# Attention and a binarised convolution on 64x64 images: other tiles summed in DRAM, the next x in eight pieces, and another order of the row products

## The chip, the cores and the metric

The kernel runs on one core of a Trainium2 chip. The core has TensorE for matmuls (PE in the profile; PEld is its weight load), VectorE (DVE), ScalarE (ACT), GpSimd (POOL), and SyncE (SP), which here only issues transfers. SP and GpSimd each have their own queue of transfers. Times are device microseconds of one execution; lower is better. The kernel before takes 1929.31 us, the median of three runs (1928.18 to 1931.14).

## The reference

Two layers work on x of shape (8, 64, 64, 64): 8 images, 64 channels, 64x64 pixels.

```python
# layer 0: attention over the n = 4096 pixels of an image
q = wq @ xf + bq;  k = wk @ xf + bk;  v = wv @ xf + bv      # per image, (64, 4096)
q, k = q - mean(q), k - mean(k)
sim = softmax(q^T k / 8, over the keys)                     # (4096, 4096)
out = sim @ v^T + (a softmax-weighted mean of v, from mean(q) and k)
x = x + out
# layer 1: three binarised convolutions (1x1, 3x3, 5x5) with batch norm, then a gate
s = sum over k in (1, 3, 5) of bn_k(conv_k(sign(x + move_k), binarised w_k))
gate = sigmoid(grouped product of mean(s) + gb), its channels shuffled
return s * gate + x
```

## The kernel before

Two images stand in the 128 partitions, so there are four pairs. The queries of a pair are cut into eight blocks of 512, so there are 32 blocks, numbered g in the order of the run. The keys are cut into 32 tiles of 128. Every matrix product is issued on quarters of the array, 64x64, so that both images and both halves of the keys are worked on together.

One block is a loop over the 32 key tiles j, and one turn of it is called a slot here. In each slot `scores` makes the 512 scores per key for both images (L491) and ACT takes their exponential into a tile e (L502); `weighted` multiplies the e of the slot before with the values and adds it to the PSUM banks acc (L510); `summed` adds that same e to the running sum es on VectorE (L526, L528), which is later needed as the softmax's denominator. The tiles e come from a pool of five buffers. One of the five is held in the first slots of a block by `parts`, the gathered sums of the block before.

Not every e is added on VectorE. For the tiles in `DRAM_TILES` (L41), `add_in_dram` (L541) sends e to a tile in DRAM instead: the first by a plain write on SP's queue (L547), the others by an accumulating transfer on GpSimd's queue (L549). At the next block's start `send` adds es in the same way, and `gather` (L554) brings the total back on SP's queue; `fold_first`, `fold`, `fold_last` reduce it on VectorE to the reciprocal, and `spread` (L581) sends it through DRAM to all partitions as r. A buffer of e is free for a new exponential only when its matmul, and its addition or its transfer, have read it.

`plan(g)` (L1079) writes by hand what else is done in which slot: `put(i, f)` calls f in slot i, after that slot's scores and the slot before's `weighted` and `summed`. Each engine works strictly in the order in which it is given its instructions. So the order of `put` calls is the order on every engine and in every queue. The work of the convolution layer is spread over the following blocks: in block g, for block g-1, `added` (the two halves of acc, L609), `finish` (times r, plus the residual, L613 and L614), and the three signs (`signs_wide` L646 for the 5x5 and 3x3, `signs` L640 for the 1x1, ACT), in slots 12 to 19; for block g-2 the combinations of rows (`row_step`, slots 17 to 24, VectorE) and their copies (`row_copies`, SP's queue); for block g-3 the products of these rows.

Those products are in `mix_rows` (L981), which runs in slot 0. It makes next block's queries (L477) and then 40 products of the 5x5 and 18 of the 3x3 for each image (L798), plus the 1x1. A product is named (k, n, tap): for the 5x5, n = 4 and 5 are the points 1/2 and -1/2, n = 0 to 3 the points 1, -1, 2, -2, n = 6 and 7 the ends. Two sequences, one for each half of the array's rows, are merged by a clock. The 3x3's products lie in the banks acc, which must have been copied out first by `weighted_out` (L535 on ACT, L536 on VectorE). `hold` (L821) brings a bank to SBUF on ACT, `join` (L830) adds another to it on VectorE. When these are done the banks go back to scores and acc.

The next pair's x is loaded by `load_x` (L67) in four transfers of 512 KB on SP's queue, all in slot 1 of the pair's third block. Its column means are taken by ACT (`mean_part`, L288) in slots 14, 16, ... 28, of the fourth block in pair 0 and of the third block in the others. In blocks five to eight of a pair the next pair's values are made (`values`, `unary_part`), two groups in each; in the eighth also `unary_sum`. In the third and fourth block the pair before is stored (`store`, L927).

Of the kernel before, what the change touches and what calls it, by code (L numbers as in the profile page):

```python
# [18 lines left out]
F32 = mybir.dt.float32  # L19
# [7 lines left out]
P = 128  # L27
C = 64
HH = 64
N = HH * HH  # L30
# [7 lines left out]
BN_EPS = 1e-5  # L38
TAPS = [[(r, c) for r in range(k) for c in range(k)] for k in KS]
FIRST = [0, 1, 10, 35]  # L40
DRAM_TILES = (4, 9, 14, 19, 24, 28)  # L41
LOW, HIGH = 1e-20, 1e20


# [1 line left out]
def conv_seq_kernel(ctx, tc, x, wq, wk, wv, vecs, w1, w3, w5, wtap, gw, out):  # L46
    nc = tc.nc
    n_pairs = x.shape[0] * x.shape[1] // P
    xf = x.rearrange("b c h w -> (b c) (h w)")
# [4 lines left out]
    xp = ctx.enter_context(tc.tile_pool(name="xp", bufs=2))  # L54
# [9 lines left out]
    def m_tile(name):  # L64
        return ps_m.tile([P, QB], F32, tag="m", name=name)

    def load_x(name, rows, queues=(nc.sync,)):  # L67
        xt = xp.tile([P, N], F32, tag="x", name=f"x_{name}")
        for c in range(4):
            cols = bass.ts(c, N // 4)  # L70
            queues[c % len(queues)].dma_start(out=xt[:, cols], in_=xf[rows, cols])
        return xt
# [12 lines left out]
    xt = load_x("0", slice(0, P), (nc.sync, nc.scalar, nc.sync, nc.sync))  # L85
# [188 lines left out]
    class Pair:  # L274
# [266 lines left out]
        def add_in_dram(self, qb, e, first=False):  # L541
            if first:
                self.sent = self.tile(dp, "es", qb, (4, 32, 4, QB // 2))
            out = self.sent.rearrange("g i q c -> (g i) (q c)")
            e = e.rearrange("p b c -> p (b c)")
            if first:
                nc.sync.dma_start(out=out, in_=e)  # L547
            else:
                nc.gpsimd.dma_start(out=out, in_=e, accum_op=ALU.add)  # L549

# [430 lines left out]
    def mix_rows(q, c):  # L981


        seqs = [[], []]
        if q is not None:
            for h in range(2):
                seqs[h].append((("q",), 0, 2.0))
        if c is not None:
            p, (r0, _, y) = c
            qb = r0 // ROWS  # L990

            def products(k, *names):
                return [((k, n), i, 0.25) for n in names for i in range(k)]

            seqs[0] += products(5, 4) + products(3, 4, 5, 0, 1, 2, 3) + [((1,), 0, 1.0)] + products(5, 5)
            seqs[1] += products(5, 0, 1, 2, 3, 6, 7)
        order = []
        for h, seq in enumerate(seqs):
            at = 0.0
            for t in seq:  # L1000
                order += [(at, h, b, t) for b in (h, 1 - h)]
                at += t[2]
        order.sort(key=lambda o: o[0:2])
        if q is not None:
            q[0].query_tiles(q[1])
        left, acc, banks5, ends = {}, None, None, None
        for o in order:
            left[o[3][0]] = left.get(o[3][0], 0) + 1
        for _, h, b, (n, i, _) in order:
            if n == ("q",):  # L1010
                q[0].split_queries(q[1], b, h)
            elif n == (1,):
                if left[n] == 2:
                    p.z1 = m_tile(f"z{p.name}_{qb}_1")
                p.conv_tap((r0, ROWS, y), [[p.z1]], b, 0, 0, 0, True, True)
            else:
                if banks5 is None:
                    banks5 = score_banks(f"z{p.name}_{qb}_5")
                if n[0] == 3:
                    if acc is None:  # L1020
                        acc = acc_banks(f"z{p.name}_{qb}_3")
                    z = acc[n[1] // 4][:, bass.ts(n[1] % 4, 2 * HH)]
                elif n[1] in (4, 5):
                    z = banks5[0][:, bass.ts(n[1] - 4, 2 * HH)]
                elif n[1] < 4:
                    z = banks5[1][:, bass.ts(n[1], 2 * HH)]
                else:
                    if ends is None:
                        ends = m_tile(f"z{p.name}_{qb}_5e")
                    z = ends[:, bass.ts(n[1] - 6, 2 * HH)]  # L1030
                p.row_product(z, b, *n, i)
            left[n] -= 1
            if left[n] > 0:
                continue
            if n == ("q",):
                q[0].split_queries_out(q[1])
            elif n == (3, 5):
                p.hold(acc[1][:, 0 : 4 * HH], 6, 2, 0)
            elif n == (3, 3):
                p.hold(acc[0], 0, 4, 0)  # L1040
        if c is not None:
            p.hold(banks5[0][:, 0 : 4 * HH], 4, 2, 2)
            p.join(ends[:, 0 : 4 * HH], 6, 2)
            p.join(banks5[1], 0, 4)

# [20 lines left out]
    def rows_of(pr):  # L1066
        return slice(pr * P, (pr + 1) * P)

    def attend(pairs):
# [9 lines left out]
        def plan(g):  # L1079
# [4 lines left out]
            def put(i, f, *a):  # L1084
                at.setdefault(i, []).append((f, a))

            pr, qb = divmod(g, NQ)

            def nx():
                return pairs[pr + 1]  # L1090
# [32 lines left out]
            if g >= 1:  # L1123
                put(5, p.fold_first, b)
                put(6, p.fold, b)
                put(7, p.fold_last, b)
                put(8, p.spread, b)
                put(9, p.check_block, b, 0)
                put(11, p.check_block, b, 1)
                put(12, p.added, b)  # L1130
                put(13, p.finish, b)
                put(15, p.signs_wide, b, 2)
                put(17, p.signs_wide, b, 1)
                put(19, p.signs, b)
            if g + 2 < n_blocks:
                put(2, lambda: block(g + 2)[0].copy_x(block(g + 2)[1], (g + 2) // NQ * P))
            if 2 <= g < n_blocks - 1:
                p2, b2 = block(g - 2)
                for i in range(5):
                    put(17 + i, p2.row_step, b2, 5, i)  # L1140
                put(21, p2.row_copies, 5)
                for i in range(2):
                    put(22 + 2 * i, p2.row_step, b2, 3, i)
                put(24, p2.row_copies, 3)
            if g == n_blocks - 4:
                put(14, p.copy_tile)
# [23 lines left out]
            if pr + 1 < n_pairs:  # L1170
                if qb == 2:
                    def begin():
                        pairs[pr + 1] = Pair(str(pr + 1), load_x(str(pr + 1), rows_of(pr + 1)))

                    put(1, begin)
                if qb == (3 if pr == 0 else 2):
                    for c in range(8):
                        cols = slice(c * QB, (c + 1) * QB)
                        put(14 + 2 * c, lambda c=c, cols=cols: nx().mean_part(c, cols, True))
                    put(30, lambda: nx().mean_sum(8))  # L1180
                if qb >= 4:
                    for h in range(2):
                        i = 2 * (qb - 4) + h
                        put(14 + 8 * h, lambda i=i: nx().values(i))
                        put(17 + 8 * h, lambda i=i: nx().unary_part(i))
                    if qb == NQ - 1:
                        put(28, lambda: nx().unary_sum())
# [6 lines left out]
        for g in range(n_blocks):  # L1194
            pr, qb = divmod(g, NQ)
# [206 lines left out]
```

## Time and profile before

| what | value |
|---|---|
| median of three runs | 1929.31 us |
| the profiled execution | 1928.91 us, its span 1927.1 us, mean granted clock 0.995 |
| idle of ACT before L502, put down to DMA es<-e | 22.9 us in 8 times, 7.6 the longest |
| idle of VectorE before L564, put down to DMA e_parts<-es | 20.5 us in 12 times |
| transfers es<-e and es<-es on GpSimd's queue | 155 and 31, 512 KB each, 5.4 us to landing (median) |
| transfers es<-e on SP's queue | 31, 512 KB each |
| x<-in_x on SP's queue | 15, 512 KB each |
| an undisturbed block (block 11) | 57.47 us: TensorE busy 57.35, VectorE 47.50, ACT 38.63 |

A line of the profile names the engine, the line of the kernel, the operation, out<-in by the names of the tiles, and how many there were. In the list of groups, the numbers after the bar are the busy time, the mean of one in ns, and then the idle time of the engine just before them with what ended it. In a list of waits the numbers are us in total, times, and the longest. In the table of stretches each row is start:end, length, and then the busy time and number of instructions of PE, PEld, DVE, ACT and POOL, the granted clock of TensorE, the share of the DMA engines' time, and GB/s. TensorE's matmuls are pipelined and overlap, so their busy time is not their number times their length.

### The profile page before, as it was taken

To read this page: it belongs to the slowest core of one execution; us is meant where nothing else is said; L and a number is where in the kernel's file an instruction comes from. 1 tells how busy PE (TensorE), PEld (TensorE's weight loads), DVE (VectorE), ACT (ScalarE), POOL (GpSimd) and SP (SyncE) were. 2 spreads that over 40 slices of the span, in tenths; PEclk is the share of its full clock that TensorE was granted. 3 is DMA by queue.
4 is the path that set the end of the run, shared out by engine and by line. 5 is a ranking of instruction groups with operands and counts; after the bars stand their busy time and mean duration, and the time that the engine had idled before them with its cause. 6 is when DMAs were issued, how large, how long until landed. Compare 5 with 4: busy or idle time off the path is not lost.

```text
span 1927.1 us, 50314 instructions
## 1 busy us (share of the span) xinstructions
PE 1891.6 (98%) x21486; PEld 798.8 (41%) x21486; DVE 1517.0 (79%) x2423; ACT 1279.8 (66%) x1639; POOL 165.7 (9%) x208
## 2 busy tenths in 40 slices
PE   9999999999998999999999999999999999999997
PEld 4333444444343344444434444334443444444444
DVE  6768877878876788787887778887887888877886
ACT  5665776666665766666666676666666666666663
POOL 0000000010000100000100001000001000001000
PEclk9999999999999999999999999999999999999999
DMA  5454444444445554444444555444444445544421
GB/s 134 80 100 99 86 83 92 87 79 83 89 88 125 95 110 83 89 92 87 69 90 85 126 109 108 81 84 88 90 90 74 87 101 109 104 91 83 85 44 46
DMA packets 80223, 174.72 MB, mean 91 GB/s; under 512 B 11180, under 2 KB 41720, under 8 KB 79864
## 3 DMA queue, kind: packets, MB, share of 16 engines
q0 software_dynamic: 26816, 97.54, 32.2%
q1 hardware_dynamic: 52456, 72.71, 12.3%
q8 instruction: 170, 2.79, 0.6%
q10 hardware_dynamic: 720, 1.18, 0.2%
q14 instruction: 61, 0.50, 0.1%
HBM read 39.27 MB, written 122.29 MB: 84 GB/s over the span
## 4 chain that ended last, share of the span: by engine, by line
PE 49%; DMA 1%; DVE 1%; ACT 0%; issue 0%; SPq 0%; ACTq 0%
PE ps L491 23%; PE acc L510 23%; DMA es<-e 1%; PE z L798 1%; DVE o L536 1%; PE z L885 0%; PE z_5e L798 0%; ACT e L502 0%; PE pv L330 0%; PE pre L1243 0%; DVE r L603 0%; ACT rc_ck L435 0%; DVE es L528 0%; SPq L468 0%; PE su L596 0%
## 5 line engine op out<-in xcount | busy, mean ns | idle before, releaser
L502 ACT ACTIVATE e<-ps 128x1024 f32<-128x1024 f32 x1024 | 1049.1, 1025 | 590.9 <-PE ps L491 549.6
L528 DVE TENSOR_TENSOR es<-es,e 128x1024 f32<-128x1024 f32 x774 | 943.8, 1219 | 265.5 <-ACT e L502 260.3
L510 PE MATMUL acc<-e,v 64*64 64x512 f32 x8192 | 1089.8, 590 | 13.1 <-ACT e L502 12.9
L491 PE MATMUL ps<-q,x 64*64 64x512 f32 x8192 | 1093.1, 591 | 3.5 <-ACT e L502 2.6
L510 PEld LDWEIGHTS acc<-e,v 64*64 64x64 f32 x8192 | 333.7, 131 | 561.3 <-ACT e L502 321.5
L491 PEld LDWEIGHTS ps<-q,x 64*64 64x64 f32 x8192 | 350.1, 133 | 489.5 <-issue 346.3
L549 POOL DMA_DIRECT2D es<-e x155 | 133.7, 863 | 1499.5 <-ACT e L502 954.9
L865 DVE SCALAR_TENSOR_TENSOR sb<-pt,sb 128x256 f32<-128x256 f32 x174 | 65.9, 420 | 0.0
L798 PE MATMUL z<-t,wc 64*64 64x128 bf16 x1392 | 60.6, 217 | 3.9 <-DVE o L536 0.5
L798 PEld LDWEIGHTS <-wc 64*64 64x64 bf16 x3364 | 58.9, 106 | 11.7 <-issue 8.2
L798 PE MATMUL z<-ec,wc 64*64 64x128 bf16 x1392 | 61.6, 217 | 0.0
L828 ACT ACTIVATE pt<-z,frac 128x256 f32<-128x256 f32 (+1 forms) x87 | 44.3, 543 | 15.6 <-PE z L798 15.6
L526 DVE TENSOR_TENSOR es<-e,e 128x1024 f32<-128x1024 f32 x32 | 39.2, 1224 | 15.6 <-ACT e L502 15.6
L646 ACT ACTIVATE s<-x,vec 128x512 bf16<-128x512 f32 (+2 forms) x66 | 46.1, 702 | 5.6 <-DVE x L614 5.6
L833 DVE SCALAR_TENSOR_TENSOR pt<-z_5e,frac,pt 128x256 f32<-128x256 f32 x29 | 14.0, 484 | 41.1 <-PE z L798 38.0
L549 POOL DMA_DIRECT2D es<-es x31 | 26.8, 863 | 172.3 <-DVE es L528 156.7
L564 DVE TENSOR_TENSOR e_parts<-e_parts 128x512 f32<-128x512 f32 x31 | 21.4, 691 | 22.0 <-DMA e_parts<-es 20.5
L536 DVE COPY o<-acc 128x512 f32<-128x512 f32 (+2 forms) x33 | 22.2, 675 | 9.6 <-PE acc L510 9.6
L839 DVE TENSOR_TENSOR pt<-pt 128x384 f32<-128x384 f32 x58 | 29.6, 552 | 0.0
L330 PEld LDWEIGHTS pv<-wx,x 64*64 64x64 f32 x1024 | 22.4, 134 | 17.0 <-issue 10.6
L613 DVE TENSOR_TENSOR x<-x,r 128x512 f32<-128x512 f32 (+2 forms) x33 | 22.2, 671 | 8.2 <-DMA r<-rc 6.0
L614 DVE SCALAR_TENSOR_TENSOR x<-x,ou,x 128x512 f32<-128x512 f32 (+2 forms) x33 | 24.3, 736 | 1.2
(177 smaller groups left out, 859.6 us busy)
## 6 DMA issues: line engine op xcount, KB each, us to landing
es<-e POOLq DMA_DIRECT2D x155, 512.0 KB, 5.4
es<-e SPq DMA_DIRECT2D x31, 512.0 KB
es<-es POOLq DMA_DIRECT2D x31, 512.0 KB, 5.4
e_parts<-es SPq DMA_DIRECT2D x124, 128.0 KB
r<-rc SPq DMA_DIRECT2D x62, 128.0 KB
x<-in_x SPq DMA_DIRECT2D x15, 512.0 KB
out<-sb SPq DMA_DIRECT2D x28, 256.0 KB
xc<-in_x SPq DMA_DIRECT2D x60, 64.0 KB
```

The lines of the kernel that those rows point to most:

```text
L491: nc.tensor.matmul(ps[img[h], b, :], self.x[img[b], bass.ds(j * P + h * H, H)], self.q[qb][img[b], :], start=True, stop=neg is None,)
L502: nc.scalar.activation(e, ps, AF.Exp, scale=1.0 / 8.0)
L510: nc.tensor.matmul(self.acc[qb][h][img[b], :], self.v[img[h], j, img[b]], e[img[h], b, :], start=(j == 0), stop=(j == NK - 1),)
L526: nc.vector.tensor_tensor(self.es[qb], self.first, e, ALU.add)
L528: nc.vector.tensor_tensor(self.es[qb], self.es[qb], e, ALU.add)
L536: nc.vector.tensor_copy(self.acc[qb][1][:, c], acc[1][:, c])
L549: nc.gpsimd.dma_start(out=out, in_=e, accum_op=ALU.add)
L646: nc.scalar.activation(sy[n][0][:, rows, pad : pad + HH], self.x2[qb][:, r0 * HH : r1 * HH].rearrange("p (h w) -> p h w", w=HH), AF.Sign, ...
L798: nc.tensor.matmul(z[img[b], :].rearrange("p (q w) -> p q w", w=HH), wc[k][img[h], n, c * C : c * C + C], src[:, first : first + step + 1 ...
L828: nc.scalar.activation(out, z, AF.Identity, scale=frac[:, by : by + 1])
L839: nc.vector.tensor_tensor(self.pairs[:, :, :, r, :], t[:, 0:3, 0], t[:, 0:3, 1], op)
L865: nc.vector.scalar_tensor_tensor(out, x, by, out, ALU.mult, ALU.add, **gap)
```

## The change

Four things change together.

- `DRAM_TILES` are 5, 11, 17 and 23 instead of 4, 9, 14, 19, 24 and 28, and the first of them is also sent by GpSimd's queue. VectorE adds two more tiles per block in 31 blocks. The last block adds all of its tiles on VectorE, before and after.
- The next x is loaded in eight transfers of 256 KB, called in slots 9, 11, ... 23 of the pair's third block, and the means are taken in the fourth block of every pair that has a next one.
- In `mix_rows` the products of n = 5 come directly after those of n = 4, ahead of the 3x3's, and the hold of their bank comes when n = 3 of the 5x5 is done, between the two holds of the 3x3.
- In `plan`, `added` moves from slot 12 to 13, `finish` from 13 to 15, the signs from 15, 17, 19 to 16, 18, 20, and the row steps one slot later, except for the last of the 3x3, which stays in 24.

```diff
-DRAM_TILES = (4, 9, 14, 19, 24, 28)
+DRAM_TILES = (5, 11, 17, 23)
...
+    def x_tile(name):
+        return xp.tile([P, N], F32, tag="x", name=f"x_{name}")
+
     def load_x(name, rows, queues=(nc.sync,)):
-        xt = xp.tile([P, N], F32, tag="x", name=f"x_{name}")
+        xt = x_tile(name)
...
             if first:
-                nc.sync.dma_start(out=out, in_=e)
+                nc.gpsimd.dma_start(out=out, in_=e)
             else:
                 nc.gpsimd.dma_start(out=out, in_=e, accum_op=ALU.add)
...
-            seqs[0] += products(5, 4) + products(3, 4, 5, 0, 1, 2, 3) + [((1,), 0, 1.0)] + products(5, 5)
+            seqs[0] += products(5, 4, 5) + products(3, 4, 5, 0, 1, 2, 3) + [((1,), 0, 1.0)]
             seqs[1] += products(5, 0, 1, 2, 3, 6, 7)
...
             elif n == (3, 5):
                 p.hold(acc[1][:, 0 : 4 * HH], 6, 2, 0)
+            elif n == (5, 3):
+                p.hold(banks5[0][:, 0 : 4 * HH], 4, 2, 2)
             elif n == (3, 3):
                 p.hold(acc[0], 0, 4, 0)
         if c is not None:
-            p.hold(banks5[0][:, 0 : 4 * HH], 4, 2, 2)
             p.join(ends[:, 0 : 4 * HH], 6, 2)
             p.join(banks5[1], 0, 4)
...
-                put(12, p.added, b)
-                put(13, p.finish, b)
-                put(15, p.signs_wide, b, 2)
-                put(17, p.signs_wide, b, 1)
-                put(19, p.signs, b)
+                put(13, p.added, b)
+                put(15, p.finish, b)
+                put(16, p.signs_wide, b, 2)
+                put(18, p.signs_wide, b, 1)
+                put(20, p.signs, b)
...
                 for i in range(5):
-                    put(17 + i, p2.row_step, b2, 5, i)
-                put(21, p2.row_copies, 5)
+                    put(18 + i, p2.row_step, b2, 5, i)
+                put(22, p2.row_copies, 5)
                 for i in range(2):
-                    put(22 + 2 * i, p2.row_step, b2, 3, i)
+                    put(23 + i, p2.row_step, b2, 3, i)
                 put(24, p2.row_copies, 3)
...
                 if qb == 2:
                     def begin():
-                        pairs[pr + 1] = Pair(str(pr + 1), load_x(str(pr + 1), rows_of(pr + 1)))
+                        pairs[pr + 1] = Pair(str(pr + 1), x_tile(str(pr + 1)))
+
+                    def load(cols):
+                        nc.sync.dma_start(out=nx().x[:, cols], in_=xf[rows_of(pr + 1), cols])
 
                     put(1, begin)
-                if qb == (3 if pr == 0 else 2):
+                    for c in range(8):
+                        put(9 + 2 * c, load, bass.ts(c, N // 8))
+                if qb == 3:
                     for c in range(8):
                         cols = slice(c * QB, (c + 1) * QB)
                         put(14 + 2 * c, lambda c=c, cols=cols: nx().mean_part(c, cols, True))
```

## The prediction

> **What bounds the kernel now.** I read the page's busy times first, then the stretches of single blocks, then the waits, then timelines of one bad block and one good one.
>
> ```profile
> PE 1891.6 (98%) x21486; PEld 798.8 (41%) x21486; DVE 1517.0 (79%) x2423; ACT 1279.8 (66%) x1639; POOL 165.7 (9%) x208
> ...
> L502 ACT ACTIVATE e<-ps 128x1024 f32<-128x1024 f32 x1024 | 1049.1, 1025 | 590.9 <-PE ps L491 549.6
> L528 DVE TENSOR_TENSOR es<-es,e 128x1024 f32<-128x1024 f32 x774 | 943.8, 1219 | 265.5 <-ACT e L502 260.3
> ```
>
> TensorE is busy 98%, so no more than the 35.5 us in which it is idle, and what it loses inside its busy time, can be won. Score and weighting matmuls alternate, and one key tile (a slot) takes 1.72 us, the pitch of ACT's exponentials below (610.27, 611.99). Stretches of whole blocks (start:end, length, busy times) show where it is more:
>
> ```profile
> 667.09:724.56 57.47, 57.35 (x642) 26.03 (x638) 47.50 (x76) 38.63 (x47) 5.17 (x6) 1.00 0.50 105
> 600.80:667.09 66.29, 59.84 (x644) 23.29 (x640) 47.75 (x80) 43.66 (x65) 5.21 (x6) 0.95 0.53 123
> 1076.78:1137.89 61.11, 58.07 (x644) 23.00 (x640) 47.85 (x80) 43.64 (x65) 5.18 (x6) 1.00 0.56 130
> 130.28:192.49 62.21, 58.04 (x526) 19.50 (x522) 51.19 (x88) 37.95 (x45) 5.18 (x6) 0.97 0.53 114
> 1254.49:1314.02 59.53, 58.66 (x706) 22.58 (x702) 47.24 (x76) 39.84 (x52) 5.17 (x6) 1.00 0.46 84
> ```
>
> The first is an undisturbed block. The next three are the third blocks of pairs 1, 2 and 0, in which the next pair's x is loaded; the fifth is one of four lesser cases (58.55 is undisturbed there, as in 309.00:367.55). The waits name the cause:
>
> ```profile
> ACT e L502 <- DMA es<-e: 22.9, 8, 7.6
> ...
> PE acc L510 <- ACT e L502: 12.9, 4, 6.3
> ```
>
> Eight times ACT wants a buffer of e from which a transfer to the DRAM sum is still reading. The worst case, in order:
>
> ```profile
> 610.27 1.02 ACT L502 ACTIVATE e<-ps 128x1024 f32<-128x1024 f32 x1 [0.36 <-PE ps L491]
> ...
> 611.12 1.85 SPq L71 DMA_DIRECT2D x<-in_x  x4
> 611.99 1.02 ACT L502 ACTIVATE e<-ps 128x1024 f32<-128x1024 f32 x1 [0.69 <-PE ps L491]
> ...
> 615.41 0.58 SPq L547 DMA_DIRECT2D es<-e  x1
> ...
> 624.00 1.94 ACT L502 ACTIVATE e<-ps 128x1024 f32<-128x1024 f32 x2 [7.61 <-DMA es<-e]
> 625.07 1.98 PE L510 MATMUL acc<-e,v 64*64 64x512 f32 x7 [6.34 <-ACT e L502]
> ```
>
> SP issues 2 MB of x, then the small xc, and only then tile 4's plain write to the sum; the write frees e 8.6 us after its issue, ACT stops 7.61 us, TensorE 6.34. The second loss is at each block's head, where the last-but-two block's row products run:
>
> ```profile
> 1606.05 0.55 PE L798 MATMUL z<-t,wc 64*64 64x128 bf16 x2
> 1606.39 0.24 PE L798 MATMUL z<-ec,wc 64*64 64x128 bf16 x1
> ```
>
> Four products start every 0.057 us (1605.81, 1605.87, 1605.92, 1605.98, 1606.04), the next group should start at 1606.09 and starts at 1606.39: the first 3x3 product needs a PSUM bank of acc, and VectorE copies it out from 1605.65 for 0.69, to 1606.34.
>
> **The skill.** The Trainium skill, "DMA: Bandwidth & Descriptors", section "SWDGE vs HWDGE vs iDMA": accumulating transfers can only be issued by GpSimd. The trace agrees as far as it goes: 186 are on POOL's queue, and the 31 plain first writes on SP's. Its section "Queues, rings and completion order": a queue's descriptors are consumed in ring order on each DMA engine, and the engine takes turns between queues. That fits the 8.6 us behind x on SP's queue, and says that a write on GpSimd's queue takes turns with x instead of standing behind it. "TensorE: Matmul & The Clock Gate", section "What's actually happening": after an idle window of some 3.4 us the clock is halved. The stretch 621:623 shows a granted clock of 0.71 and 623:625 of 0.50, so the stall of 6.34 cost more than itself. Price: "VectorE: DVE Perf Modes", section on the errata, gives (N+151)/0.96 ns for a float32 tensor_tensor, 1224 ns at 1024; the row has 1219.
>
> **The change, part by part.**
>
> *Stalls of e that go.* Against undisturbed blocks of the same kind: 66.29-57.95 = 8.3 and 61.11-57.95 = 3.2 (57.95 is 1546.81:1604.76, the last pair's third block, which has stores and gate but no load); the four lesser cases 59.01, 59.46, 59.47, 59.53 against 58.55 give 3.3. In pair 0's third block, one-time weight work hides the base; ACT's starts there are 3.9 and 1.9 late at tiles 8 and 10, 5.8 together. Sum 20.6 us. SP's tile write, which stood behind the gather, x and xc, no longer exists, and x comes after r in 256 KB pieces. The lesser cases are tile 9's accumulate meeting r's broadcast; the transfers of tiles 11, 17 and 23 stand clear of it, and finish is two tiles later, so the 6.0 us that VectorE waits for r (4 times) go too; no separate gain, the same blocks.
>
> *What stays late there.* In pair 0's third block finish now comes after the weight combinations of tile 14 (five, about 0.4 each), and the signs one tile after it instead of two; ACT, in order, waits in front of the exponentials. By adding VectorE's queue from tile 12 I get finish some 1.6 us too late: +2.0 with the six pieces of x issued at once there. In the other two, pieces and stores share the engines with the accumulates: 0.3 each. Stall gain 18.0 us; bounds 12 and 20.6.
>
> *Tile 5's write on GpSimd.* Its e must be free at tile 9, four slots later (tile 10 for the others is one slot more). GpSimd issues 1.31 us after the exponential starts (1564.80 to 1566.11 for tile 9), so 4x1.72-1.31 = 5.6 us are left, and 0.3 more before TensorE feels it. A plain write there is not in the trace. Above: an accumulate's landing, 5.4 median of 5.1 to 8.1. Below: SP's queue moves 72.7 MB in 12.3% of the span, 1.6 us per 512 KB; GpSimd's 97.5 MB in 32.2%, 3.3 per accumulate; so 5.4-3.3+1.6 = 3.7 us. I take 3.7, and no stall. GpSimd has 5 issues per block for 6; its order is as before, each accumulate waiting for the one before, 10 us apart.
>
> *Two more additions.* 62x1.22 = 75.6 us on VectorE. An undisturbed block has 10.0 us of its idle time, 2.4 are taken. It costs only if VectorE is still behind when acc must be copied out. Tiles 24 to 31 are now summed without a break: eight additions of about 1.32 back to back leave 0.4 per slot, 3.2 in all, and 0.5 more where the next pair's values run. Against that: what is left of the row steps (0.8), in the second half of a pair the unary part (1.4), in its last block the unary sum (1.4). It just fits; 0.5 us in four blocks, taken as 1 together; bounds 0 and 12 (0.4 in every block).
>
> *Means on ACT.* For pairs 2 and 3 they move to the fourth block, and in all three such blocks the signs at tiles 16, 18 and 20 now share a slot with a mean (14+2c); before, they alternated. ACT has 0.69 free per slot; signs 0.71 and mean 0.71 overrun by about 0.5, of which 0.35 is covered by e being ready early. 9x0.15 = 1.3 us lost.
>
> *Row products.* Ten units instead of five (40 products for 20) precede the first 3x3: 1605.81+10x0.057 = 1606.38, against 1606.39. So 0.29 is won, unless its end gives it back. There the hold of the 1/2 and -1/2 products moves ahead of the 3x3's 512-wide hold on ACT; that one ended at 1608.33 and would end at about 1608.39, while the first weighting matmul, at 1608.71 now, would want its bank at 1608.42. VectorE's joins and the next scores move with TensorE. I take 0.25 in each of 29 blocks: 7.2 us; bounds 0 and 8.7. One unknown fewer: the moved products need only banks and copies that the first 5x5 products need already.
>
> *No effect:* eight DMA issues of x for four (SP is not waited for; ec and y behind them have six slots and a block), signs one slot later.
>
> Sum: -18.0+1.0+1.3-7.2 = -22.9. The profiled run took 1928.9 (span 1927.1 and 1.8 around it); it lies 0.4 under the median of 1929.3. So 1906.0 on its own footing, 1906.4 on the median's; I say 1906.
>
> **Rivals.**
> (a) The mix gives nothing: ACT's reordered holds set when acc is free. For it: that bank was already waited for (a 0.3 us weight-load wait on ACT's hold, 28 times). Against: its computed end moves by 0.06 only. 1906+7 = 1913.
> (b) VectorE becomes the bound at block ends. For: 79% rises to 83%, no break after tile 23. Against: 1.5 to 2 us of idle in the last slots of the fullest blocks. At 0.4 us in each block, 1917.
> (c) Slower: tile 5's landing. If a plain write through GpSimd lands no sooner than an accumulate that meets other traffic, at 7 us, ACT is 1.4 late and TensorE 1.1 in each of 31 blocks: +34, so 1940. It loses against before from about 6.7 us on, and the gather of the sums ends just ahead of it. Against: 5.4 is the median even of accumulates, and the write moves half as long.
> (d) The pieces of x don't do what is said: SP reaches them late or in one burst, and the load blocks keep half their stalls: 1914.
>
> **Chances.** Forecast 0.58 (1901 to 1911), (a) 0.12, (b) 0.12, (c) 0.08, (d) 0.10. 0.2% is 3.9 us, about the least that a measurement of this kernel tells from no change. Faster 0.87, same 0.05 (the worse end of b), slower 0.08. The range 1899 to 1915 leaves out (c), half of (b), and a little at the lower end.
>
> **What would show it.** Right: no wait of ACT on es<-e over 1 us, third blocks within 2 us of 58; GpSimd's plain write landing under 4.5 us; blocks of 57.2 instead of 57.47, with no gap in the row products; fourth blocks about 0.5 longer than that; 836 additions. Wrong: a wait at tile 9 in every block (c); VectorE's copy of acc starting late at block heads (b); the first weighting matmul waiting for ACT's hold (a).

## The result, and the profile after

The changed kernel takes 1904.86 us, the median of four runs (1904.70 to 1905.70), beside 1928.74 for the kernel before, measured with it. The ratio is 0.9876, its 95% interval 0.9859 to 0.9893: 1.2% faster. The profiled execution took 1904.84 us, span 1903.1.

Lines of the page after: busy times of the engines, GpSimd's queue (packets, MB, share of the DMA engines' time), VectorE's additions, and GpSimd's two kinds of transfers of e to the sum (accumulates, then plain writes).

```profile
PE 1884.7 (99%) x21486; PEld 752.1 (40%) x21486; DVE 1588.6 (83%) x2485; ACT 1275.3 (67%) x1639; POOL 129.1 (7%) x177
...
q0 software_dynamic: 22352, 81.29, 24.1%
...
L531 DVE TENSOR_TENSOR es<-es,e 128x1024 f32<-128x1024 f32 x836 | 1019.6, 1220 | 196.7 <-ACT e L505 183.4
...
L552 POOL DMA_DIRECT2D es<-e x93 | 80.0, 860 | 903.2 <-ACT e L505 599.8
...
L550 POOL DMA_DIRECT2D es<-e x31 | 17.3, 558 | 340.4 <-ACT e L505 329.1
```

There are 62 more additions, as computed, and VectorE's busy time rises by 71.6 us, while the time falls by 24. An engine's busy sum does not tell this; what counts is where TensorE stood. The lines of the kernel are three higher up to line 930: L505 is the exponential that was L502.

Stretches of whole blocks (start:end, length, busy times and numbers of PE, PEld, DVE, ACT, POOL, clock, DMA share, GB/s): an undisturbed block (block 9, since block 11 now has the means), the third and the fourth block of pair 1 (blocks 10 and 11), the third blocks of pairs 0 and 2 (blocks 2 and 18), and one of the lesser cases (block 21).

```profile
538.90:596.09 57.19, 57.19 (x642) 22.48 (x638) 47.22 (x74) 38.51 (x47) 3.99 (x5) 1.00 0.34 69
596.09:653.77 57.68, 57.68 (x644) 22.12 (x640) 50.12 (x81) 38.75 (x49) 3.98 (x5) 1.00 0.50 123
653.77:711.14 57.37, 57.37 (x642) 21.72 (x638) 49.88 (x79) 43.02 (x63) 3.99 (x5) 1.00 0.39 87
130.98:190.02 59.04, 56.58 (x526) 19.78 (x522) 53.10 (x90) 37.92 (x45) 4.00 (x5) 1.00 0.44 102
1059.83:1117.50 57.67, 57.67 (x644) 22.12 (x640) 50.11 (x81) 38.74 (x48) 3.99 (x5) 1.00 0.51 123
1233.63:1291.91 58.28, 58.28 (x706) 22.95 (x702) 49.72 (x78) 39.82 (x52) 3.99 (x5) 1.00 0.34 68
```

An undisturbed block is 57.19 us instead of 57.47. The third block of pair 1 is 57.68 instead of 66.29, that of pair 2 57.67 instead of 61.11, and TensorE is busy in all of it at full clock (0.95 before in the worst). Of these, only pair 0's third block (59.04) still has TensorE idle, 59.04-56.58 = 2.5 us. The waits of TensorE, VectorE and ACT after (total, times, longest) say the same:

```profile
PEld acc L513 <- ACT pt L831: 18.3, 29, 0.6
...
DVE e_parts L567 <- DMA e_parts<-es: 8.1, 7, 1.5
...
ACT s L649 <- DVE x L617: 7.7, 3, 3.9
...
PE acc L513 <- ACT e L505: 1.9, 2, 1.6
...
ACT e L505 <- DMA es<-e: 0.9, 1, 0.9
```

ACT's wait for a buffer of e went from 22.9 us in 8 times to 0.9 in one; VectorE's wait for the gathered sums from 20.5 to 8.1. VectorE's wait for r, 6.0 us before, is gone.

Block by block the two traces add up. The stalls: block 10 gives 8.6, block 18 3.4, block 2 3.2, the four lesser cases 0.7 to 1.3 each; less the 0.28 that the 29 blocks from block 3 on win alike at their heads (six of these seven are among them, all but block 2), 17.9. The 0.28 is 8.1 in all. On the other side: the three fourth blocks with means 0.2 each, block 1 0.4, what follows the last exponential of the last block 0.8 (30.43 instead of 29.64), the start 0.35. So -17.9-8.1+0.6+0.4+0.8+0.35 = -23.85, and the spans differ by 24.0.

### Where the wins and the small losses lie

The timeline of pair 1's third block (start, length, engine, line, operation, count, idle time before), cut to ACT's exponentials and the transfers that matter:

```profile
608.32 0.56 POOL L550 DMA_DIRECT2D es<-e  x1 [10.50 <-ACT e L505]
...
613.67 1.11 SPq L589 DMA_DIRECT2D r<-rc  x2
...
614.83 1.52 SPq L1180 DMA_DIRECT2D x<-in_x  x3
615.52 1.03 ACT L505 ACTIVATE e<-ps 128x1024 f32<-128x1024 f32 x1 [0.36 <-PE ps L494]
```

Tile 5's plain write is issued before any piece of x, which waits on SP behind the two transfers of r and comes 6.5 us later. The transfers of that line land like this over the whole run (min, median, max):

```profile
DMA to landing us min/median/max: 2.9/2.9/3.4
```

That is 2.9 us against the budget of 5.6. It is never late. The pieces of x do not come one by one: SP had waited for r, and three go out together (six in pair 0).

The block head in pair 3's fourth block, after:

```profile
1582.12 0.69 DVE L539 COPY o<-acc 128x512 f32<-128x512 f32 x1 [0.32 <-PE acc L513]
...
1582.81 0.27 PE L801 MATMUL z<-t,wc 64*64 64x128 bf16 x2
1582.87 0.24 PE L801 MATMUL z<-ec,wc 64*64 64x128 bf16 x1
...
1583.43 1.42 ACT L831 ACTIVATE pt<-z,frac 128x256 f32<-128x256 f32 x3 [0.32 <-PE z L801]
...
1584.90 0.22 PEld L513 LDWEIGHTS acc<-e,v 64*64 64x64 f32 x8 [0.64 <-ACT pt L831]
```

The ten groups of 5x5 products now last to 1582.81, when VectorE's copy of acc ends (1582.12+0.69); the 3x3 products follow without a gap. At the other end the weights of the first weighting matmul wait 0.64 for ACT's hold, which in the kernel before was 0.30: the hold now decides when the head ends, but it does so at 3.68 us after the first exponential of the block against 3.95 (1584.91-1581.23; 1608.71-1604.76 before).

The remaining loss, in pair 0's third block:

```profile
160.03 0.48 DVE L263 SCALAR_TENSOR_TENSOR wc<-wt 128x320 bf16<-128x320 bf16 x1
160.55 0.89 DVE L265 SCALAR_TENSOR_TENSOR wc<-wc 128x320 bf16<-128x320 bf16 x2
...
161.36 1.22 DVE L531 TENSOR_TENSOR es<-es,e 128x1024 f32<-128x1024 f32 x1
...
162.50 0.68 DVE L616 TENSOR_TENSOR x<-x,r 128x512 f32<-128x512 f32 x1
163.22 0.75 DVE L617 SCALAR_TENSOR_TENSOR x<-x,ou,x 128x512 f32<-128x512 f32 x1
...
164.00 0.72 ACT L649 ACTIVATE s<-x,vec 128x512 bf16<-128x512 f32 x1 [2.05 <-DVE x L617]
164.63 1.00 ACT L505 ACTIVATE e<-ps 128x1024 f32<-128x1024 f32 x1
```

Read it from the bottom: the exponential at 164.63 stands behind the signs, which stand behind `finish` (L616, L617), which stands on VectorE behind an addition and the weight combinations (L263, L265). ACT stood idle for 2.05 us, for some 1.6 of them with the scores of its next exponential made (their matmuls run from 161.32 to 162.36). The one wait for e that is left also lies in this block: the exponential at 160.92 waited 0.91 us for tile 11's accumulate, which was issued just after the six pieces of x and took 7.3 us to land. It came only 0.2 us late by that.

### The profile page after: what moved, and what is told of

It is laid out like the page before. It is cut to its first block, busy times and chain, and to the rows that moved or that the text cites. A ratio compares the mean times of both kernels' runs of the same rounds, so it can differ in the third digit from the quotient of the medians.

```text
span 1903.1 us, 50293 instructions
## 1 busy us (share of the span) xinstructions
PE 1884.7 (99%) x21486; PEld 752.1 (40%) x21486; DVE 1588.6 (83%) x2485; ACT 1275.3 (67%) x1639; POOL 129.1 (7%) x177
## 2 busy tenths in 40 slices
DMA packets 73024, 142.22 MB, mean 75 GB/s; under 512 B 10380, under 2 KB 40920, under 8 KB 72664
## 3 DMA queue, kind: packets, MB, share of 16 engines
q0 software_dynamic: 22352, 81.29, 24.1%
## 4 chain that ended last, share of the span: by engine, by line
PE 97%; DMA 1%; DVE 1%; ACT 1%; issue 0%; SPq 0%; ACTq 0%
PE ps L494 46%; PE acc L513 46%; PE z L801 2%; PE pv L333 1%; PE pq L480 1%; PE z L888 0%; PE z_5e L801 0%; DMA x<-in_x 0%; DMA es<-es 0%; ACT e L505 0%; PE warm L155 0%; PE pre L1252 0%; DVE r L606 0%; DMA e_parts<-es 0%; DVE es L531 0%
## 5 line engine op out<-in xcount | busy, mean ns | idle before, releaser
L505 ACT ACTIVATE e<-ps 128x1024 f32<-128x1024 f32 x1024 | 1048.5, 1024 | 572.5 <-PE ps L494 559.2
L531 DVE TENSOR_TENSOR es<-es,e 128x1024 f32<-128x1024 f32 x836 | 1019.6, 1220 | 196.7 <-ACT e L505 183.4
L494 PE MATMUL ps<-q,x 64*64 64x512 f32 x8192 | 1077.5, 590 | 0.9 <-DVE kb L165 0.9
L513 PE MATMUL acc<-e,v 64*64 64x512 f32 x8192 | 1074.9, 590 | 2.2 <-ACT e L505 1.9
L513 PEld LDWEIGHTS acc<-e,v 64*64 64x64 f32 x8192 | 315.1, 131 | 568.0 <-ACT e L505 313.1
L494 PEld LDWEIGHTS ps<-q,x 64*64 64x64 f32 x8192 | 327.7, 133 | 510.3 <-issue 256.7
L552 POOL DMA_DIRECT2D es<-e x93 | 80.0, 860 | 903.2 <-ACT e L505 599.8
L801 PEld LDWEIGHTS <-wc 64*64 64x64 bf16 x3364 | 54.6, 106 | 4.8 <-issue 0.7
L801 PE MATMUL z<-ec,wc 64*64 64x128 bf16 x1392 | 52.1, 217 | 0.0
L801 PE MATMUL z<-t,wc 64*64 64x128 bf16 x1392 | 51.5, 217 | 0.2 <-DVE o L539 0.2
L550 POOL DMA_DIRECT2D es<-e x31 | 17.3, 558 | 340.4 <-ACT e L505 329.1
L617 DVE SCALAR_TENSOR_TENSOR x<-x,ou,x 128x512 f32<-128x512 f32 (+2 forms) x33 | 24.3, 736 | 1.2
```

What stands on the lines that cost most here:

```text
L494: nc.tensor.matmul(ps[img[h], b, :], self.x[img[b], bass.ds(j * P + h * H, H)], self.q[qb][img[b], :], start=True, stop=neg is None,)
L505: nc.scalar.activation(e, ps, AF.Exp, scale=1.0 / 8.0)
L513: nc.tensor.matmul(self.acc[qb][h][img[b], :], self.v[img[h], j, img[b]], e[img[h], b, :], start=(j == 0), stop=(j == NK - 1),)
L531: nc.vector.tensor_tensor(self.es[qb], self.es[qb], e, ALU.add)
L801: nc.tensor.matmul(z[img[b], :].rearrange("p (q w) -> p q w", w=HH), wc[k][img[h], n, c * C : c * C + C], src[:, first : first + step + 1 ...
```

## Experiments

The ratios are to the kernel before as it ran beside each experiment, with medians of 1929.43 to 1930.38 us. The kernel after was not run beside them again, so medians that differ from its 1904.86 by one or two us do not decide anything by themselves; the lengths of single blocks in the traces do, where they repeat.

**Undo the order of the row products** in the kernel after; all else stays.

```diff
-            seqs[0] += products(5, 4, 5) + products(3, 4, 5, 0, 1, 2, 3) + [((1,), 0, 1.0)]
+            seqs[0] += products(5, 4) + products(3, 4, 5, 0, 1, 2, 3) + [((1,), 0, 1.0)] + products(5, 5)
...
-            elif n == (5, 3):
-                p.hold(banks5[0][:, 0 : 4 * HH], 4, 2, 2)
...
         if c is not None:
+            p.hold(banks5[0][:, 0 : 4 * HH], 4, 2, 2)
```

> The changed kernel with the row products and the hold in their old order; all else is kept. My theory (the 3x3's products wait 0.3 us for VectorE's copy of acc, and ten units of the 5x5 ahead of them cover it): every block from the fourth on is 0.28 us longer again, 29 x 0.28 = 8.1 us, so 1913.0 us; slot 0 lasts 4.25 us instead of 3.97, with a gap in the row products before the first 3x3. Rival (the shorter slot 0 comes from VectorE's copy being on time because the tiles and steps moved): slot 0 stays at 3.97 and the time near 1905.

Measured: 1912.94 us (1912.33 to 1913.10), ratio to before 0.9922 (0.9904 to 0.9939). The 29 heads from block 3 on are 0.28 longer again (4.25 us from the first exponential to the second instead of 3.97; in block 30 instead of 4.07). In the timeline of the same head, the copy of acc and the start of the 3x3 products:

```profile
1588.92 0.69 DVE L539 COPY o<-acc 128x512 f32<-128x512 f32 x1 [0.32 <-PE acc L513]
...
1589.33 0.55 PE L801 MATMUL z<-t,wc 64*64 64x128 bf16 x2
...
1589.67 0.24 PE L801 MATMUL z<-ec,wc 64*64 64x128 bf16 x1
```

The copy ends at 1589.61, the product starts at 1589.67, and the product before it is drawn out to 0.55: the gap is back. The order is worth 8 us, and rival (a) is out.

**The new order alone** in the kernel before: the same edit, the other way round.

> The kernel before with only the order of the row products and the hold changed. My theory: slot 0 of 29 blocks falls from 4.25 to 3.97 us, and the stalls on e in the third blocks and at tile 9 stay: 1928.7 - 8.1 = 1920.6 us. Rival (the order only shifts work to the next wait, and it paid in the changed kernel because VectorE's schedule changed as well): under 3 us of gain.

Measured: 1925.27 us (1920.53 to 1929.17, 16 runs), ratio 0.9973 (0.9963 to 0.9983). This is 5.1 us under the kernel before as it ran beside it (1930.38, 19 runs); 8.1 were expected, and the rival said under 3. In the profiled execution 26 of the 29 heads have the 0.28; the other three take 4.90 (block 19), 4.29 (block 28) and 4.18 us (block 30) instead of 3.97. So the mechanism holds without the rest, but not all of its gain arrives. The start is 2.4 us later (first exponential at 17.01 instead of 14.62), and the blocks in which x is loaded differ from those of before: 62.83, 65.25 and 63.60 instead of 62.21, 66.29 and 61.11, where each would have been expected the same or shorter. Why they came out so was not tried. A stall from colliding transfers is not a constant: the runs of this kernel spread over 8.6 us (16 runs) and those of before over 10.9 (19 runs), those of after over 1.0 (four runs).

**x at once**: in the kernel after, the next x in four transfers of 512 KB in slot 1.

```diff
-                    for c in range(8):
-                        put(9 + 2 * c, load, bass.ts(c, N // 8))
+                    for c in range(4):
+                        put(1, load, bass.ts(c, N // 4))
```

> The changed kernel with the next x loaded as before: four transfers of 512 KB in slot 1 of the third block, on SP's queue; tiles, queue, order and means stay as changed. Theory A (the stall came from the tile's write standing behind 2 MB of x in SP's queue; on GpSimd's queue it takes turns with x): the third blocks of pairs 0 to 2 grow by 0 to 2 us each, all together under 4 us, so 1905 to 1909. Theory B (the DMA engines are full of x, whichever queue the tile's write is on): tile 5's write lands several us late, each third block loses 3 us or more, 1914 or above.

Measured: 1910.88 us (1909.20 to 1914.25), ratio 0.9911 (0.9889 to 0.9933): 6.0 us of the gain are lost. Pair 1's third block in its timeline, and the two waits of the whole run:

```profile
605.38 1.90 SPq L1180 DMA_DIRECT2D x<-in_x  x4
...
609.36 0.56 POOL L550 DMA_DIRECT2D es<-e  x1 [10.50 <-ACT e L505]
```

```profile
ACT e L505 <- DMA es<-e: 9.8, 3, 3.5
```

Tile 5's write, on GpSimd's queue, was issued 2.1 us after the last of x's issues and landed 8.05 us after its issue (7.43 in pair 0's load block, 8.17 in pair 2's), where it lands in 2.9 elsewhere. Behind x on SP's queue, in the kernel before, it was 8.6 us from the write's issue to the exponential that waited for it (7.4 and 7.1 in the other two). So the other queue did not protect the transfer itself. The loss was 2.3 and 4.0 us in pairs 1 and 2 and 0.7 in pair 0, 7.0 in all, between the two expectations and about half of the 15.2 that these blocks had gained. What the queue wins here is the issue: GpSimd issued 0.3 us after tile 5's exponential (608.03+1.02 to 609.36), SP, with the issues of x and xc ahead, 4.1 us after tile 4's (610.27+1.02 to 615.41). That the issue accounts for the other half is read from these two timelines; this kernel also has other tiles and slots than the kernel before, and x at once with the write on SP's queue was not run with them. The landing agrees with the Trainium skill, "DMA: Bandwidth & Descriptors", section "Issuing engines are not separate DMA queues": transfers run on the same 16 DMA engines whichever engine issued them.

**The first write on SP's queue**, with the pieces of x where after has them.

```diff
             if first:
-                nc.gpsimd.dma_start(out=out, in_=e)
+                nc.sync.dma_start(out=out, in_=e)
```

> The changed kernel with the first tile of each block written on SP's queue again, and x still in eight later pieces. Theory A (SP's queue hurt only because x was ahead of it): tile 5's write comes after gather and xc, both long issued by slot 5, so no stall comes back: 1904 to 1906, no wait of ACT on es<-e over 1 us. Rival (the queue itself matters: SP's waits for the gather and for r delay the issue): ACT waits at tile 9 in several blocks, over 3 us in all.

Measured: 1905.83 us (1904.96 to 1906.30), ratio 0.9884 (0.9867 to 0.9902), 1.0 above after. Third blocks of pairs 0, 1 and 2: 59.03, 57.67, 57.67, as after. It costs at most about 1 us, and none of the stalls of before comes back. ACT does wait for e twice, 1.58 us in pair 0's third block and 1.24 in block 28, both times for tile 11's accumulate; more than the 1 us that was expected at most, and neither is a wait for the write. SP issues the write 0.03 us after tile 5's exponential, sooner than GpSimd's 0.3. What keeps the write from standing behind x is that x comes later, not the queue.

**x alone**: the kernel before with x in eight pieces and the means in the fourth block; tiles, slots and order as before.

```diff
...
-                        pairs[pr + 1] = Pair(str(pr + 1), load_x(str(pr + 1), rows_of(pr + 1)))
+                        pairs[pr + 1] = Pair(str(pr + 1), x_tile(str(pr + 1)))
...
+                    def load(cols):
+                        nc.sync.dma_start(out=nx().x[:, cols], in_=xf[rows_of(pr + 1), cols])
...
-                if qb == (3 if pr == 0 else 2):
+                    for c in range(8):
+                        put(9 + 2 * c, load, bass.ts(c, N // 8))
+                if qb == 3:
```

> The kernel before with only the load of x changed: eight transfers of 256 KB in slots 9 to 23 of the third block, means in the fourth block. Six tiles, SP's write, the order of products and the slots of finish and the signs are as before. My theory (x in front of the tile's write made the large stalls): the three third blocks lose their 3.2 to 8.3 us of stall, together 15 to 17 us, and the lesser waits at tile 9, 3.3 us in all, stay: 1912 to 1915 us. The means do not collide with the signs, which are in odd slots there. Rival (four tiles on GpSimd's queue were what removed the stalls): at most 6 us are won, 1922 or above.

Measured: 1912.22 us (1910.78 to 1914.55), ratio 0.9903 (0.9886 to 0.9920). The third blocks are 57.40, 57.95 and 58.23: the large stalls are gone. Three of the four lesser cases stay (59.05, 59.43, 59.54), and so do short waits:

```profile
ACT e L505 <- DMA es<-e: 10.7, 9, 1.7
```

This tells what the rest of the change does. The kernel with the old order (first experiment) and this one differ by the tiles, the write's queue and the slots of `added` to the row steps. Block by block these three together win 0.5, 0.9, 1.0 and 0.3 in blocks 7, 15, 21 and 18, and lose 0.4, 1.6 and three times 0.2 in block 1, block 2 and the fourth blocks: +2.6 and -2.6. Which of the three does what was not separated. The net is nothing, though the whole program moves 32.5 MB less (142.22 instead of 174.72 between before and after). The large stalls came from where x lay, and with x gone from there the DMA engines' load set little more.

**Three tiles in DRAM** (5, 12, 19) instead of four.

```diff
-DRAM_TILES = (5, 11, 17, 23)
+DRAM_TILES = (5, 12, 19)
```

> The changed kernel with three tiles (5, 12 and 19) summed in DRAM, so one more addition of 1.22 us on VectorE in 31 blocks. It asks how much room VectorE has left. My theory (VectorE is behind at no block's head but the second's, with some 1 to 4 us to spare): under 6 us lost, 1905 to 1911, the losses in the last block of a pair. Rival (VectorE is at its bound with four tiles already): each block's head is late by up to 1.2 us, 20 us or more lost.

Measured: 1906.78 us (1906.09 to 1909.16), ratio 0.9881 (0.9865 to 0.9898). Every block is as after or up to 0.1 shorter, except pair 0's third block with 61.09 (59.04 after) and blocks 19 and 28, 0.2 longer. The last blocks of the pairs, where the losses were expected, lose nothing.

**Two tiles in DRAM** (11, 23), two additions more per block than after.

> The changed kernel with two tiles (11 and 23) in DRAM: two more additions, 2.44 us, on VectorE in 31 blocks. VectorE is idle 9.97 - 2.4 = 7.5 us in an undisturbed block with four tiles, 5.1 with two. If only its total counted nothing would be lost; if its position at finish (a wait of ACT before the signs) and at the block's end counts, as I hold, it loses at these two places: 1 to 2 us in most blocks, 1925 to 1970. Rival (VectorE is off the path): 1905 to 1908.

Measured: 1907.60 us (1907.20 to 1909.54), ratio 0.9885 (0.9868 to 0.9901). My own expectation fell: VectorE was to become the bound in most blocks. Pair 0's third block and an undisturbed block in the table of stretches:

```profile
130.95:192.70 61.75, 58.28 (x526) 20.20 (x522) 55.56 (x92) 37.92 (x45) 2.27 (x3) 0.97 0.31 81
541.39:598.57 57.18, 57.18 (x642) 22.47 (x638) 49.22 (x76) 38.52 (x47) 2.28 (x3) 1.00 0.23 51
```

The undisturbed block is as short as after, with VectorE busy two microseconds more. The loss lies in pair 0's third block, 2.7 us (61.75-59.04); no other block is over 0.25 longer.

This block shows something about x as well. The first tile sent to DRAM is now 11, and its plain write on GpSimd's queue follows six pieces of x; the last line gives the landings of all 31 such writes:

```profile
151.06 2.95 SPq L1180 DMA_DIRECT2D x<-in_x  x6
...
153.48 0.56 POOL L550 DMA_DIRECT2D es<-e  x1 [20.81 <-ACT ck L438]
...
DMA to landing us min/median/max: 2.9/2.9/7.4
```

The 7.4 is this write, as late as those that met x in four large transfers. Cutting x up does not protect a write when six pieces go out just ahead of it.

**Move what collides**: in the kernel after, the two late weight combinations go from slots 14 and 16 to 17 and 19, and the means to odd slots, away from the signs.

```diff
-                    put((9, 11, 14, 16, 26, 28, 29)[i], f)
+                    put((9, 11, 17, 19, 26, 28, 29)[i], f)
...
-                        put(14 + 2 * c, lambda c=c, cols=cols: nx().mean_part(c, cols, True))
-                    put(30, lambda: nx().mean_sum(8))
+                        put(15 + 2 * c, lambda c=c, cols=cols: nx().mean_part(c, cols, True))
+                    put(31, lambda: nx().mean_sum(8))
```

> The changed kernel with the means in slots 15, 17, ... 29 instead of 14, 16, ... 28, and two steps of weight combinations in pair 0's third block in slots 17 and 19 instead of 14 and 16. My theory: the means no longer share a slot with a sign (three blocks, 0.2 us each, 0.6 together), and finish is no longer 2 us late in the third block (2.0 to 2.5 us): 1902.0 to 1902.7 us in place of 1904.9. Rival (the third block's stall is x's six pieces landing on tile 11's accumulate): the block keeps its 2 us, and the time stays within 1 us of 1904.9.

Measured: 1904.08 us (1903.63 to 1905.64), ratio to before 0.9866 (0.9850 to 0.9882). Its pair 0's third block, the one after it, and pair 1's fourth block:

```profile
131.02:188.21 57.19, 56.34 (x526) 19.88 (x522) 52.57 (x89) 38.06 (x44) 4.00 (x5) 1.00 0.45 105
188.21:245.81 57.60, 57.35 (x642) 22.49 (x638) 47.92 (x76) 43.40 (x64) 4.00 (x5) 1.00 0.34 69
652.16:709.35 57.19, 57.19 (x642) 22.47 (x638) 49.80 (x79) 43.41 (x64) 4.09 (x5) 1.00 0.39 87
```

Both losses are gone: 59.04 becomes 57.19, and 57.38 becomes 57.19. The places were right, and the six pieces of x, which still go out together there, were not the cause. But 1902.0 to 1902.7 was expected, and the median is 1.4 above that. The moved combinations make VectorE late at the end of their block instead, and the next head gives back 0.4 (57.60 against 57.19). Blocks 15 and 21 are 0.3 longer than after and the heads of blocks 28 to 30 0.2 to 0.4; VectorE's copy of acc is on time in these heads, they vary in other kernels too (block 28 is 57.68 in the fourth experiment), and their cause was not followed. By its median this is the fastest of these kernels, but the 0.8 us from after lie inside the spread of the runs, so whether it beats after is open.

**How far VectorE can be filled**: the moves of the last experiment with two tiles in DRAM (11, 23), and with one (17).

```diff
-DRAM_TILES = (5, 11, 17, 23)
+DRAM_TILES = (11, 23)
```

> The moves of e8 with two tiles summed in DRAM (11 and 23), so that VectorE has four additions more per block than in the kernel before and two more than after. Theory: what e7 lost against after was one place, pair 0's third block, where the weight combinations and finish share VectorE; the moves take most of it away and VectorE has room everywhere else. Then within 1.5 us of e8: 1903.5 to 1905.6, pair 0's third block under 59 (61.75 in e7). Rival: VectorE is now full at the block heads behind crowded blocks, which e8 showed in small; then another 0.3 to 0.5 in some ten blocks, 1907 to 1909.

> The moves of e8 with a single tile (17) summed in DRAM, one addition more per block than with two. It looks for the point at which VectorE becomes the bound. The undisturbed block has 47.2 us of VectorE in 57.2 after; three additions more are 3.7, so 50.9; the third blocks 53.8. Theory of room: still only pair 0's third block and its neighbours lose, 1904 to 1908. Rival (VectorE the bound at block ends): heads late in most blocks, 0.5 to 1.2 in 29 blocks, 1920 to 1940.

Measured: 1904.92 us (1904.49 to 1905.09) with two tiles, ratio 0.9874 (0.9856 to 0.9892), and 1907.49 (1905.85 to 1909.71) with one, ratio 0.9885 (0.9867 to 0.9903). With two, pair 0's third block is 57.98 instead of 61.75, as expected, but the head after it is 1.8 late, which was not. With one, VectorE is busy 89% of the span; its third and fourth blocks of pair 1:

```profile
599.85:657.52 57.67, 57.67 (x644) 22.11 (x640) 53.23 (x84) 38.79 (x48) 1.42 (x2) 1.00 0.35 96
657.52:714.71 57.19, 57.19 (x642) 22.47 (x638) 53.17 (x82) 43.41 (x63) 1.42 (x2) 1.00 0.22 60
```

They are as short as with four tiles, with 53.2 us of 57.2 busy on VectorE. Most of what is lost lies in pair 0's third block (59.31) and above all at the head behind it, where the additions run late and the copy of acc behind them (blocks 15, 21, 24, 28 and 29 lose another 0.2 to 0.5 each):

```profile
191.09 3.88 DVE L531 TENSOR_TENSOR es<-es,e 128x1024 f32<-128x1024 f32 x3
...
194.88 0.68 DVE L539 COPY o<-acc 128x512 f32<-128x512 f32 x1
...
195.62 0.21 PE L801 MATMUL z<-t,wc 64*64 64x128 bf16 x1 [1.61 <-DVE o L539]
```

The block's first exponential is at 192.22, so the copy starts 2.66 us after it instead of 0.89 as in the head shown of after, and TensorE waits 1.61 for it. That is rival (b) as it was described, but at this head, where the eighth experiment showed 0.4 of it, and with one tile in small at block 24's (a copy 0.4 late, 0.35 us lost). At all other heads but block 1's the copy is on time, with two or three additions per block more than after. (The profiled executions of these two kernels are 4.6 us apart, of which 2.0 is the start: first exponential at 16.95 with one tile, 14.90 with two.)

## Why the prediction was right

The time was 1904.86 against 1906.0, inside the range and, but for what protects the write from x, on the forecast's own mechanism. By its steps:

- *The stalls that go.* Said: 20.6 gross, 2.6 staying, so 18.0. Measured: 17.9. The parts differ a little. In pair 0's third block the gross was 5.0 and not 5.8 (62.21 before, 57.19 in the version in which the wait is taken out), and 1.85 stayed where 2.0 was said, for the reason given: `finish` behind the weight combinations, and ACT's signs behind `finish` (the eighth experiment takes this away, and the block is 57.19). The 0.3 in each of the other two third blocks did not come: 57.67 is 57.95 less the 0.28 of the order. The lesser cases are gone in the first experiment (58.55 and 58.56, without the 0.28) and three of four stay in the fifth, so the tiles, the queue and the slots together end them.
- *What ends the large stalls* was put down to x coming late and in pieces and to the write having left SP's queue. The runs split the two: x alone ends them (fifth experiment); the rest of the change without it leaves half of them (third), and with x moved the queue is not needed (fourth). That a write on another queue takes turns with x instead of standing behind it did not show as protection here: 7.4, 8.05 and 8.2 us against 7.4, 8.6 and 7.1. On this point the prediction had the right result for a wrong reason. Whether it is the later moment or the cutting into pieces that does it was not tried apart; the seventh experiment speaks for the moment.
- *Tile 5's write*: said 3.7 us to landing, measured 2.9 with 3.4 the longest. The estimate added an accumulate's whole overhead, 5.4-3.3 = 2.1, to a moving time of 1.6 (worked like the 3.3 it is 1.7). GpSimd's queue after took 24.1% of the span, 459 us; less 124 accumulates at 3.34 each (32.2% of 1927.1 us over 186, before), 414 us, that leaves about 1.5 us for each of 31 plain writes, an estimate. So most of the miss is the overhead, some 1.4 instead of 2.1. Rival (c) needed 6.7 and had no place in this kernel; in the third experiment, where x meets the write, it is reached in three blocks.
- *Two more additions*: said 1.0, bounds 0 to 12. At block heads it is 0.4, in block 1, where VectorE's copy of acc comes 0.4 later. From block 3 to block 30 the last addition of a block ends 0.56 us after the next block's first exponential, before and after alike: VectorE has caught up by then. With three additions more per block again, no block but the one behind pair 0's third is more than 0.6 longer than after. So rival (b) was further off than the working had it: "it just fits" was too cautious.
- *Means and signs in one slot*: said 1.3, from 0.15 for each of nine. Measured 0.19 per block, 0.6 in all, as this timeline of ACT in a fourth block after shows:

```profile
683.54 1.02 ACT L505 ACTIVATE e<-ps 128x1024 f32<-128x1024 f32 x1 [0.74 <-PE ps L494]
684.46 0.71 ACT L649 ACTIVATE s<-x,vec 128x512 bf16<-128x512 f32 x1
685.07 0.62 ACT L294 ACTIVATE mean<-x 128x512 bf16<-128x512 f32 x1
...
685.68 1.01 ACT L505 ACTIVATE e<-ps 128x1024 f32<-128x1024 f32 x1
686.98 1.02 ACT L505 ACTIVATE e<-ps 128x1024 f32<-128x1024 f32 x1 [0.29 <-PE ps L494]
```

 The exponential starts 2.14 after the one before instead of 1.72, so it is 0.42 late, and the next follows after 1.30: ACT's usual wait for scores, 0.74 above, shrinks to 0.29 and takes it up. In the block's next two collisions the next turn makes up all but the 0.19. The term was twice too large.
- *Row products*: said 0.25 in 29 blocks, 7.2; measured 0.28, 8.1, so next to nothing was given back at the end, although ACT's hold did become what the first weighting matmul waits for. It ends 3.62 us after the block's first exponential (1583.43+1.42-1581.23), where the prediction's figures give 3.63.
- Not in the sum: the start, 0.35 us later, and the end of the last block, 0.8 longer (30.43 us behind the last exponential, 29.64 before). As far as the runs tell neither belongs to the change: the fourth and the eighth experiment, with the same additions, have 29.93 there, and the start varies by more between kernels in which nothing near it was changed.

Sized wrongly, then, were the additions by -0.6, the means by -0.7 and the products by -0.9, the stalls by +0.1, and +1.15 were left out: -0.95 together, against the 1.1 between forecast and measurement. That the total came so close is in part luck: the terms of the sum are off by 2.1 us, and the start and the end of the program took back half of it.

## What to carry to other kernels

Lay a bulk load where no buffer's release depends on a transfer of that moment. Another queue does not keep a small transfer out of its way, and pieces that go out together do not either; the same edit done alone shows which of two such steps does the work. Before fearing the fuller engine, look for the one block in which something else is queued ahead of the instruction that others wait for: most of the losses from more VectorE work that could be placed sat there or at the head behind it. And where an engine in a steady pattern is late by less than its partner's lead, the loss is mostly made good in the next turn, so charge a collision only for what it exceeds that lead by.

## What was not expected of the hardware

- A plain write of 512 KB from SBUF to DRAM issued by GpSimd lands 2.9 us after its issue (31 times, 2.9 to 3.4), an accumulating one of the same size 5.3 to 5.4 (medians by tile); issuing takes GpSimd 0.56 us and 0.86.
- That same write takes 7.4 to 8.2 us when 2 MB of loads were issued shortly before on SP's queue (third experiment), and 7.4 behind six loads of 256 KB (seventh).
- The start of the same work varies: the first exponential came at 14.6 to 15.3 us in nine of the profiled executions and at 16.9 to 17.0 in three, with edits that do not touch it.
